# Spectral filters of a two-layer model: one 128 x 128 matrix per frequency, for all four elements together

## The chip, the core and the metric

The kernel runs on one core of a Trainium2 chip. A core has engines that run beside each other, each from its own queue in order: TensorE (PE, matrix products; the loads of its weights are shown apart as PEld), VectorE (DVE), ScalarE (ACT), GpSimd (POOL) and SyncE (SP), which here issues every DMA. PE writes to PSUM, eight banks of 512 f32 a partition; ACT or DVE copy the results out ("evict" them). All data are f32. The metric is the time of one execution on the device, in microseconds, lower being better, as the median of several runs. A profile of one execution comes with it.

## The reference, cut to what matters

The input is 4 elements ("b") of 64 x 64 positions with 128 channels. Layer 0 is a convolutional state-space block: a projection, a 3 x 3 depthwise convolution, and selective scans along four directions (256 channels, 16 states, 4096 positions each), followed by a gated norm and a projection; then a router with 64 experts. Layer 1 mixes rows and columns, and then applies spectral filters to a normed sequence `u` of 4096 positions:

```python
Vf = jnp.fft.rfft(phi, n=n, axis=0)                  # n = 8192, 16 filters
Uf_p = jnp.fft.rfft(u, n=n, axis=1)
U_plus = jnp.fft.irfft(Vf[None, :, :, None] * Uf_p[:, :, None, :], n=n, axis=1)[:, :sl]
...
out = jnp.einsum('btkd,k,kde->bte', U_plus, s, Mpp)
out = out + jnp.einsum('btkd,k,kde->bte', U_minus, s, Mpm)
```

`U_minus` is the same with every second position of `u`, and of the result, negated. So for one frequency the sum over the 16 filters and over plus and minus is one product of `u`'s spectrum (128 channels) with one complex 128 x 128 matrix, which is the same for all four elements. Four such mixtures with a Gumbel choice are added; the choice turns into a weight for each position (`wpj`, `wseg`).

## The kernel before, in words

The time is filled by the scans. An outer loop over `s` has 2048 steps: 4 elements x 4 directions x 8 chunks of 512 positions x 16 states. One step is: a broadcast load of B and C (`bc`, L1461, SP), two exponentials of 512 (`da`, L1471, ACT), a product of 1024 (`db`, L1501, DVE), two scans of 512 (`hh`, L1507, DVE), a product with C of 1024 (L1517, POOL), and eight transposes on PE that add up in PSUM (`y`, L1543).

The rest of the model is written as generators ("pieces") that yield a weight after each piece. `deal` puts pieces between the scan's instructions, twice a step, with manual dependencies that hold them at their place in each engine's queue. `WEIGHT[b]`, the total for an element, spread over all deals, sets how much is dealt at a time; `LAG` is a weight that stands for waiting. What is not yet dealt when an element's scans end is run out in a lump. `beside(b)` (L1312) lists what goes beside the scans of element b:

- b = 0: `before_scans` of elements 1, 2, 3 (norm, projection, depthwise convolution), `gate` of 0, 1, 2, and `filters` (weights of the mixture, matrices `me` and `mo`, spectra of `phi`).
- b = 1, 2, 3: for element b - 1 the stages `after_scans`, `experts_and_sums` and `to_slots` (called front stages below), and then `convolve` for 8 of the 64 groups of slots.

`to_slots(b)` (L1094) takes a short discrete Fourier transform over blocks of positions (PE, `fu_ps`, L1106) and stores the slots to DRAM (`ud`). Even and odd positions are kept apart. `convolve` (L1117) then does within each slot what the rest of a full transform would do, as a Toeplitz product: for every group of 4 slots, in four parts, it loads `slab` (the filters' values, 1 MB a part), multiplies it with `us` (PE, `cv_ps`, L1170, 64 rows, two at a time), evicts to `y`, multiplies with the 16 matrices `me` and `mo` (PE, `zq_ps`, L1191), adds the halves on POOL, turns the result (`zt_ps`, L1213) and stores it to `zd`. `from_slots(b)` (L1238) goes back (PE, `gi_ps`, L1268), scales by `wpj` and adds to `x3`, which is the output.

PSUM: the scan holds six banks for `du`, `db` and `y`; the pieces have the two others, as two single ones (`slots(2, 0)`) or, for `convolve`, as one pair (`slots(0, 1)`, `pair`).

After the last scan comes the tail. The front stages of element 3 are run there with groups 24 to 47 of `convolve` beside them, by a ratio of 3.2, in an order of PE's queue written out by hand (`behind`); then `from_slots` of 1 and 2 and the first loads of 3's with the last 16 groups; then the rest of 3's.

## Time and profile before

| | us |
|---|---|
| median of 3 runs (10947.52 to 10952.77) | 10948.95 |
| span of the profiled execution | 10931.4 |
| DVE busy (75%) | 8233.2 |
| PE busy (79%), weight loads PEld (45%) | 8642.8, 4876.0 |
| POOL busy (62%), ACT busy (57%) | 6817.4, 6232.6 |
| HBM read 1766.77 MB, written 205.52 MB | 180 GB/s over the span |

The profiled execution is one run with the profiler on; its span lies 17.6 us under the median. A line such as "L1507 DVE TENSOR_TENSOR_SCAN hh<-da,hst,db 128x512 f32 x3584 | 4392.8, 1266" says: line 1507, engine, operation, what it writes and reads, the shape, how many; busy time in us, mean ns of one. An f32 matmul leaves two records of PE, and two of PEld. Busy shares are means over stages with different limits; which wait ends last in a stage says what bounds it.

### The profile page before, as it was taken

How to read it: one execution, taken by the hardware profiler on the slowest of the kernel's cores; microseconds unless marked ns; L12 is line 12 of the kernel's file. 1: busy time of each engine (PE TensorE's matmuls, PEld its weight loads, DVE VectorE, ACT ScalarE, POOL GpSimd, SP SyncE). 2: the span in 40 equal slices, each digit the busy share in tenths (PEclk: the TensorE clock that was granted, in tenths of full speed). 3: DMA queues.
4: the chain of work that ended last, by engine and by line, in shares of the span. 5: the costliest groups of instructions: out<-in, count | busy, mean ns of one | idle time of the engine just before them, and what ended most of it. 6: DMA issues, size and time to landing. Idle time of an engine off the chain costs nothing. (4 is left out here: it accounts for less than half of the span.)

```text
span 10931.4 us, 119319 instructions
## 1 busy us (share of the span) xinstructions
PE 8642.8 (79%) x35936; PEld 4876.0 (45%) x35936; DVE 8233.2 (75%) x7094; ACT 6232.6 (57%) x12156; POOL 6817.4 (62%) x6102
## 2 busy tenths in 40 slices
PE   6787777657786777768777777787777799999999
PEld 2444444434454444445543344455344444445443
DVE  0888989988998999989989899798899922222322
ACT  4767676758576655675755557657556544134221
POOL 1777777987777887877777788677788711001000
PEclk9788888768888888878888888788788899999999
DMA  2455656657756666657565567575666565544554
GB/s 94 167 194 181 208 182 213 211 187 222 236 191 205 187 195 189 216 166 270 167 193 179 170 194 229 167 255 161 197 199 189 174 165 129 143 126 107 137 134 118
DMA packets 901464, 1980.28 MB, mean 181 GB/s; under 512 B 101562, under 2 KB 415578, under 8 KB 899290
## 3 DMA queue, kind: packets, MB, share of 16 engines
q1 hardware_dynamic: 900826, 1972.65, 59.2%
q8 instruction: 293, 4.80, 0.2%
q14 instruction: 345, 2.83, 0.1%
HBM read 1766.77 MB, written 205.52 MB: 180 GB/s over the span
## 5 line engine op out<-in xcount | busy, mean ns | idle before, releaser
L1517 POOL TENSOR_TENSOR hh<-hh,bc 128x1024 f32<-128x1024 f32 x2048 | 4885.4, 2386 | 413.6 <-DVE hh L1507 177.0
L1507 DVE TENSOR_TENSOR_SCAN hh<-da,hst,db 128x512 f32<-128x512 f32 x3584 | 4392.8, 1266 | 487.8 <-PE y L1543 134.6
L1471 ACT ACTIVATE da<-dl,aneg 128x512 f32<-128x512 f32 x4096 | 2765.9, 717 | 1845.2 <-DVE hh L1507 1769.7
L1543 PE MATMUL y<-ident,hh 128*128 128x128 f32 x16384 | 2605.4, 307 | 552.8 <-POOL hh L1517 474.7
L1543 PEld LDWEIGHTS y<-ident,hh 128*128 128x128 f32 x16384 | 2169.9, 159 | 1914.6 <-issue 1012.9
L1501 DVE TENSOR_TENSOR db<-du,bc 128x1024 f32<-128x1024 f32 x1920 | 2365.4, 1232 | 178.6 <-ACT du L1452 76.9
L1170 PE MATMUL cv_ps<-slab,us 64*128 64x512 f32 x4096 | 1162.1, 673 | 519.9 <-ACT y L257 277.7
L257 ACT COPY y<-cv_ps 128x512 f32<-128x512 f32 (+1 forms) x1024 | 755.9, 743 | 718.4 <-PE cv_ps L1170 703.1
L1516 POOL COPY hst<-hh 128x2 f32<-128x2 f32 x1792 | 381.4, 213 | 1065.8 <-DVE hh L1507 961.1
L1191 PE MATMUL zq_ps<-y,me 128*128 128x512 f32 x2048 | 998.4, 608 | 38.6 <-ACT y L257 35.3
L1191 PE MATMUL zq_ps<-y,mo 128*128 128x512 f32 x2048 | 975.9, 600 | 0.0
L1207 POOL TENSOR_TENSOR zt<-zt,zt 128x512 f32<-128x512 f32 x64 | 81.1, 1268 | 1205.9 <-DVE zt L255 608.8
L1170 PEld LDWEIGHTS cv_ps<-slab,us 64*128 64x128 f32 x4096 | 397.0, 201 | 974.3 <-ACT y L257 368.4
L255 DVE COPY y<-cv_ps 128x512 f32<-128x512 f32 x640 | 441.4, 691 | 508.3 <-PE cv_ps L1170 456.6
L1507 DVE TENSOR_TENSOR_SCAN hh<-da,db 128x512 f32<-128x512 f32 x512 | 596.7, 1207 | 41.8 <-PE y L1543 8.8
L411 PE MATMUL cv_ps<-xh,diag 128*128 128x512 f32 x1152 | 524.9, 598 | 9.4 <-ACT dl L1396 9.1
L1191 PEld LDWEIGHTS zq_ps<-y,me 128*128 128x128 f32 x2048 | 350.8, 193 | 368.1 <-issue 261.1
L1191 PEld LDWEIGHTS zq_ps<-y,mo 128*128 128x128 f32 x2048 | 359.1, 192 | 318.7 <-issue 316.6
L1361 PE MATMUL dt_ps<-dts,dtw 8*128 8x512 f32 x512 | 352.1, 801 | 160.7 <-ACT zt L257 45.3
L1501 DVE TENSOR_TENSOR db<-dx,bc 128x1024 f32<-128x1024 f32 x128 | 210.8, 1647 | 332.4 <-POOL dx L1403 319.6
L1387 POOL TENSOR_TENSOR ex<-ex,dx 128x1024 f32<-128x1024 f32 x128 | 302.5, 2363 | 159.8 <-ACT dx L1384 146.6
L255 DVE COPY zt<-zq_ps 128x512 f32<-128x512 f32 x42 | 29.0, 691 | 491.4 <-PE zq_ps L1191 491.4
(235 smaller groups left out, 9283.9 us busy)
## 6 DMA issues: line engine op xcount, KB each, us to landing
bc<-bc_d SPq DMA_DIRECT2D x2048, 512.0 KB
slab<-hd SPq DMA_DIRECT2D x1024, 256.0 KB
xc<-xc_d SPq DMA_DIRECT2D x128, 512.0 KB
y_d<-ys SPq DMA_DIRECT2D x128, 512.0 KB
w1t<-in_w_dram SPq DMA_DIRECT2D x128, 512.0 KB
w2t<-in_w_dram SPq DMA_DIRECT2D x256, 256.0 KB
xc_x<-xc_d SPq DMA_DIRECT2D x64, 512.0 KB
yk<-y_d SPq DMA_DIRECT2D x128, 256.0 KB
```

Source lines behind the costliest of these rows:

```text
L255: nc.vector.tensor_copy(dst, src)
L257: nc.scalar.copy(dst, src)
L411: nc.tensor.matmul(ps, diag[:, h, t, :], xh[:, 8 * g + dy : 8 * g + dy + 8, dx : dx + W], start=(t == 0), stop=(t == 8),)
L1170: nc.tensor.matmul(pq[q].rearrange("p (r k t) -> p r k t", r=2, t=BS), us[b, G][rows, p, a if e == 0 else 1 - a, :], slab[i][rows, p, :, : ...
L1191: nc.tensor.matmul(z, (me, mo)[e][:, KQ * kq + k, :], ys[e][:, :, :, :, k, :].rearrange("p a q r t -> p (a q r) t"), start=(e == 0 and k = ...
L1361: nc.tensor.matmul(ps, dtw[:, k, h * P : (h + 1) * P], dts, start=True, stop=True)
L1471: i_act = nc.scalar.activation(das[t][:, h, :], sizes[t // N][0][:, h, :], AF.Exp, scale=aneg[:, tk, h, t % N : t % N + 1],)
L1501: nc.vector.tensor_mul(db, src, bcs[s][:, 0:1, :].to_broadcast([P, 2, SC]))
L1507: i_dve = nc.vector.tensor_tensor_scan(o, d0, d1, init, ALU.mult, ALU.add)
L1516: nc.gpsimd.tensor_copy(hsts[t // N][:, :, t % N], hhs[t][:, :, last])
L1517: i_pool = nc.gpsimd.tensor_mul(hhs[t], hhs[t], bcs.pop(t)[:, 1:2, :].to_broadcast([P, 2, SC]))
L1543: i_pe = nc.tensor.matmul(ys[c][:, q, h, :], hhs[t][:, h, q * P : (q + 1) * P], ident, is_transpose=True, start=(n == 0 and k > 0 and q % ...
```

## The change

The blocks of even and odd positions are given up. One transform of 8192 points is split in two: over 64 blocks of 64 positions (as before in `to_slots`, now 64 slots of both halves), and within a slot over its 64 positions by a matrix with the twiddle factors in it (`fq`, `gq`, from `_twiddled`, stored in DRAM, 4.2 and 8.4 MB). `filters` now also turns the 32 matrices `me`, `mo` and stores them (`md`), and stores the filters' full spectra (`vd`, 32 x 64 x 128).

`convolve` and `from_slots` are gone, and with them the pair of banks, `behind` and the ratios. Beside the scans there are only front stages: `before_scans(3)` goes from element 0's scans to element 2's, the gates each an element ahead of their use, and `WEIGHT` is set to what these stages' own weights sum to, which is dealt over the whole of an element's scans. In the tail the front stages of element 3 run alone. Behind them, with the weights' memory freed, comes `spectrum`: for two slots at a time (`FB`, 32 iterations) it

- loads `vt`, `u1` and `fq` and transforms all four elements (`forward`),
- makes the two slots' 2 x 64 complex matrices from 32 filters (`taps_of`): 128 products of 32 rows x 256 columns, on four row groups of the array; 32 evictions of 1024, stored with a step of 512 bytes to `wt` (one buffer, 128 KB a partition),
- multiplies (`product`): 128 products with 32 columns of weights (4 frequencies x real and imaginary x 4 elements, of which 8 rows are used) and 256 columns moving, on four column groups; 8 evictions of 1024 to `zs` (one buffer), and 16 DMAs of 64 KB to `zf`,
- loads `zf` again in another order (`load_back`) and transforms back (`backward`), to `zd`.

`endings` does what `from_slots` did, for all elements at once. PSUM is held by `spectrum` as four pairs of banks. The diff follows, with the old lines of the functions that went left out:

```diff
@@ -32,47 +32,70 @@
 
 
 FIRST = 1
-WEIGHT = (1346.0, 2080.0, 1999.0, 2052.0)
+WEIGHT = (972.0, 1008.0, 1346.0, 927.0)
 
 BUSY = (2, 3)
 
 LAG = 5.0
 
-BESIDE = 8
-
-
-BS = 32
-NB = HALF // BS
+BP = 64
+NB = L // BP
 NQ = NB
-KQ = 8
+KK = 2 * KF
+FB = 2
...
-    zd = [dram.tile([NQ, 2, BS, 2, C], F32, name=f"zd{b}") for b in range(B)]
-
-    HDQ = 2 * 2 * 2 * 2 * KQ * 2 * BS
-    hd = dram.tile([NQ * HDQ + 2 * BS], F32, name="hd")
+    ud = dram.tile([NQ, 2 * BP, B, C], F32, name="ud")
+    zf = dram.tile([NQ, 2, BP, 2 * B, C], F32, name="zf")
+    zd = dram.tile([NQ, 2, BP, B, C], F32, name="zd")
+    vd = dram.tile([KK, NQ, 2 * BP], F32, name="vd")
+    md = dram.tile([KK, C, C], F32, name="md")
 
     ident = const.tile([P, P], F32, name="ident")
     make_identity(nc, ident)
...
+                me = fp.tile([P, 4, C], F32, name="me")
+                mo = fp.tile([P, 4, C], F32, name="mo")
+                nc.gpsimd.tensor_add(me, accp[:, ks], accm[:, ks])
+                nc.gpsimd.tensor_sub(mo, accp[:, ks], accm[:, ks])
+                for i in range(4):
                     for m in (me, mo):
+                        nc.scalar.activation(
+                            m[:, i], m[:, i], AF.Identity, scale=sg[:, k + i : k + i + 1]
+                        )
                 yield 3.0
+                for a, m in enumerate((me, mo)):
+                    ps = bank([P, 4, C], "mt_ps")
+                    for i in range(4):
+                        nc.tensor.transpose(ps[:, i, :], m[:, i, :], ident)
+                    mT = fp.tile([P, 4, C], F32, name="mT")
+                    evict(mT, ps)
+                    nc.sync.dma_start(
+                        md[a * KF + k : a * KF + k + 4].rearrange("k e d -> e k d"), mT
+                    )
+                    yield 2.0
...
+            for q in range(0, NQ, 4):
+                fr = hp.tile([BP, 4, 2, 2 * BP], F32, name="fr", bufs=3)
+                for i in range(4):
+                    nc.sync.dma_start(
+                        fr[:, i], fq_d[q + i].rearrange("(r p) n -> p r n", p=BP)
+                    )
+                ps = bank([KK, 4, 2 * BP], "v_ps")
+                for i in range(4):
+                    for r in range(2):
                         nc.tensor.matmul(
+                            ps[:, i, :],
+                            hs[:, q + i, r, :],
+                            fr[:, i, r, :],
+                            start=(r == 0),
+                            stop=(r == 1),
+                        )
+                vs = hp.tile([KK, 4, 2 * BP], F32, name="vs")
+                evict(vs, ps)
+                nc.sync.dma_start(vd[:, q : q + 4, :], vs)
+                yield 2.0
...
+    def spectrum():
+
+        with tc.tile_pool(name="sp", bufs=2) as sp, tc.tile_pool(
+            name="sp_ps", bufs=4, space=PSUM
+        ) as sps:
+            taps = sp.tile([P, C // 8, 2, C], F32, name="taps", bufs=1)
+            for g in range(4):
+                nc.sync.dma_start(
+                    taps[g * KK : (g + 1) * KK],
+                    md.rearrange("k (j g i) d -> k j g i d", g=4, i=2)[:, :, g],
+                )
+            wt = sp.tile([P, FB * 2 * BP, C], F32, name="wt", bufs=1)
+            u1, fq, vt, ut, zq, gq = {}, {}, {}, {}, {}, {}
+            side["e"] = 0
+
+            def banks():
+                return sps.tile([P, 2, 512], F32, name="sp_ps", tag="ps")
+
+            def out(dst, src):
+                side["e"] += 1
+                (nc.scalar.copy if side["e"] % 2 else nc.vector.tensor_copy)(dst, src)
+
+            def load(i):
+                vt[i] = sp.tile([P, FB, 2 * BP], F32, name="vt")
+                for g in range(4):
+                    nc.sync.dma_start(vt[i][g * KK : (g + 1) * KK], vd[:, FB * i : FB * (i + 1)])
+                for q in range(FB * i, FB * (i + 1)):
+                    u1[q] = sp.tile([P, B, C], F32, name="u1")
+                    nc.sync.dma_start(u1[q], ud[q])
+                    fq[q] = sp.tile([P, 2 * BP], F32, name="fq")
+                    nc.sync.dma_start(fq[q], fq_d[q])
+
+            def forward(i):
+                ps = banks()
+                ut[i] = sp.tile([P, FB, BP, 2, B], F32, name="ut")
+                for s in range(FB):
+                    q = FB * i + s
+                    for b in range(B):
+                        nc.tensor.matmul(
+                            ps[:, s, b * 2 * BP : (b + 1) * 2 * BP],
+                            u1[q][:, b, :],
+                            fq[q],
+                            start=True,
+                            stop=True,
+                        )
+                    out(
+                        ut[i][:, s].rearrange("d m u b -> d b (m u)"),
+                        ps[:, s].rearrange("d (b n) -> d b n", b=B),
                     )
 
+            def taps_of(i):
+                for j in range(C // 8):
+                    pair = [banks(), banks()]
+                    for t in range(2):
+                        for g in range(4):
+                            rows = slice(g * KK, (g + 1) * KK)
                             nc.tensor.matmul(
+                                pair[g // 2][:, g % 2, t * 256 : (t + 1) * 256],
+                                taps[rows, j, t, :],
+                                vt[i][rows].rearrange("k s n -> k (s n)"),
                                 start=True,
                                 stop=True,
                             )
+                    for h in range(2):
+                        e = 8 * j + 4 * h
+                        out(
+                            wt[:, :, e : e + 4].rearrange("d n e -> d e n"),
+                            pair[h].rearrange("d g (t n) -> d (g t) n", t=2),
+                        )
+
+            def product(i):
+                for s in range(FB):
+                    q = FB * i + s
+                    zs = sp.tile([P, BP // 4, 2, C], F32, name="zs", bufs=1)
+                    for m in range(0, BP // 4, 4):
+                        ps = banks()
+                        for k in range(4):
+                            w0 = ut[i][:, s, 4 * (m + k) : 4 * (m + k) + 4]
+                            for g in range(4):
+                                n = 2 * (s * BP + 4 * (m + k) + g)
+                                nc.tensor.matmul(
+                                    ps[32 * g : 32 * g + 32, k // 2, (k % 2) * 256 :][:, 0:256],
+                                    w0.rearrange("d m u b -> d (m u b)"),
+                                    wt[:, n : n + 2, :].rearrange("d w e -> d (w e)"),
+                                    start=True,
+                                    stop=True,
+                                )
+                        out(
+                            zs[:, m : m + 4].rearrange("z m w e -> z (m w e)"),
+                            ps.rearrange("z k n -> z (k n)"),
+                        )
+                    for g in range(4):
+                        for w in range(2):
+                            nc.sync.dma_start(
+                                zf[q, w].rearrange("(m g) z e -> z g m e", g=4)[:, g],
+                                zs[40 * g : 40 * g + 8, :, w, :],
+                            )
+
+            def load_back(i):
+                for q in range(FB * i, FB * (i + 1)):
+                    zq[q] = sp.tile([P, 2, B * C], F32, name="zq")
+                    for w in range(2):
+                        nc.sync.dma_start(
+                            zq[q][:, w], zf[q, w].rearrange("m (u b) e -> (m u) (b e)", u=2)
+                        )
+                    gq[q] = sp.tile([P, 2, 2 * BP], F32, name="gq")
+                    nc.sync.dma_start(gq[q], gq_d[q])
+
+            def backward(i):
+                ps = banks()
+                zo = sp.tile([P, FB, B * C], F32, name="zo", bufs=1)
+                for s in range(FB):
+                    q = FB * i + s
+                    for w in range(2):
                         nc.tensor.matmul(
+                            ps[:, s, :], gq[q][:, w, :], zq[q][:, w, :], start=(w == 0), stop=(w == 1)
+                        )
+                out(zo, ps)
+                for s in range(FB):
+                    nc.sync.dma_start(
+                        zd[FB * i + s].rearrange("r p b e -> (r p) (b e)"), zo[:, s, :]
+                    )
+
+            n = NQ // FB
+            load(0)
+            load(1)
+            forward(0)
+            for i in range(n):
+                if i >= 1:
+                    load_back(i - 1)
+                taps_of(i)
+                if i + 1 < n:
+                    forward(i + 1)
+                if i + 2 < n:
+                    load(i + 2)
+                if i >= 1:
+                    backward(i - 1)
+                product(i)
+            load_back(n - 1)
+            backward(n - 1)
...
             def turn(g):
                 for t in range(4):
+                    ps = gps.tile([NB, B * C], F32, name="gi_ps", tag="ps")
+                    nc.tensor.matmul(ps, gi_t, zb[g][:, t, :], start=True, stop=True)
+                    xt = xr[g][:, t].rearrange("j b c -> j (b c)")
+                    nc.vector.scalar_tensor_tensor(xt, ps, wpj, xt, ALU.mult, ALU.add)
...
     def beside(b):
 
         if b == 0:
-            for i in range(1, B):
-                yield from before_scans(i)
-            for i in range(B - 1):
-                yield from gate(i)
+            yield from before_scans(1)
+            yield from before_scans(2)
+            yield from gate(0)
+            yield from gate(1)
             yield from filters()
-        else:
-            yield from after_scans(b - 1)
-            yield from experts_and_sums(b - 1)
-            yield from to_slots(b - 1)
-            if b == 1:
-                yield from gate(B - 1)
-            if b == B - 1:
-                yield from from_slots(0)
-            yield from convolve(all_groups[BESIDE * (b - 1) : BESIDE * b])
+            return
+        if b == 2:
+            yield from before_scans(3)
+        yield from after_scans(b - 1)
+        yield from experts_and_sums(b - 1)
+        yield from to_slots(b - 1)
+        if b < B - 1:
+            yield from gate(b + 1)
...
     side["tail"] = True
-    slots(8, 0)
...
+    slots(8)
+    run(after_scans(B - 1))
+    run(experts_and_sums(B - 1))
+    run(to_slots(B - 1))
+    side.pop("pool").close()
+    weights.close()
+    spectrum()
+    endings()
```

## The prediction

> **What bounds the kernel now.** I read the page first, then busy time by stage, then the chain of waits, and at the end single tiles. The page's slices (each digit a tenth, 273 us a slice) show two regimes.
>
> ```profile
> PE   6787777657786777768777777787777799999999
> ...
> DVE  0888989988998999989989899798899922222322
> ```
>
> For 32 slices DVE is nearly full; in the last eight DVE falls to 2 and PE stands at 9. The stages come from the scan's own instructions: an element starts at 295, 2370, 4472, 6613 us, and the last scan ends at 8746. Busy time by stage (length, then PE, PEld, DVE, ACT, POOL, clock, DMA share, GB/s), and one quiet stretch:
>
> ```profile
> 295.00:2370.00 2075.00, 1519.12 (x6024) 917.18 (x6024) 1899.20 (x1560) 1419.90 (x2631) 1647.08 (x1324) 0.81 0.59 194
> 2370.00:4472.00 2102.00, 1586.92 (x7453) 971.04 (x7452) 1912.24 (x1561) 1365.06 (x2590) 1665.72 (x1435) 0.85 0.65 201
> 4472.00:6613.00 2141.00, 1588.80 (x7380) 966.37 (x7380) 1921.67 (x1562) 1328.68 (x2523) 1650.10 (x1422) 0.84 0.62 194
> 6613.00:8746.00 2133.00, 1613.32 (x7455) 984.04 (x7456) 1917.54 (x1560) 1327.93 (x2523) 1658.69 (x1449) 0.85 0.63 197
> 8746.00:10931.00 2185.00, 2130.63 (x7175) 953.68 (x7173) 578.03 (x828) 659.50 (x1577) 159.82 (x395) 0.99 0.53 132
> ...
> 8001.00:8680.00 679.00, 515.67 (x2180) 284.08 (x2180) 646.62 (x529) 412.62 (x590) 560.65 (x386) 0.88 0.63 191
> ```
>
> In the quiet stretch convolution pieces run beside the scan and DVE is busy 95%: 176 steps (three DVE instructions each) in 679 us, 3.858 us a step, 61.7 us a chunk of 16. So the filters beside the scans cost the scan nothing, and taking them out gives nothing there. At that rate 128 chunks are 7898 us, but the scans took 8746 - 295 = 8451: 553 us of stalls. They lie beside the front stages. Two samples of the waits (us in total, times, longest), 5495 to 5570 us beside `to_slots`, and 2670 to 2770 us beside the router:
>
> ```profile
> PE fu_ps L1106 <- DMA ub<-u_d: 9.7, 1, 9.7
> ...
> DVE hh L1507 <- PE y L1543: 16.9, 4, 5.8
> ...
> DVE hh L1507 <- ACT da L1471: 23.5, 5, 8.2
> ```
>
> A dealt piece waits at the head of PE or ACT for its own input; the scan's transposes or exponentials queue behind it, then DVE stops. In the tail the chain of waits is PE alone:
>
> ```profile
> 10784.63 13.93 PE zq_ps L1191 x32
> ```
>
> 32 records of 512 columns in 13.93 us: 0.435 us each, 0.85 ns a column, two records for each f32 matmul.
>
> **What the Trainium skill says.** (1) TensorEngine Tiling (Array Packing), Key Properties: tiles of the array run in parallel, a change of tiling mode drains. Before agrees for two tiles: `cv_ps` (64 rows) keeps PE busy 1162.1/4096 = 0.284 us a record against 998.4/2048 = 0.487 for `zq_ps` of full height. Four are in no row of before. (2) TensorE: Matmul & The Clock Gate, Measured speedup vs the span model: four row tiles gave 3.07x, three column tiles 2.38x. (3) The tiling page, PSUM Bottleneck: evacuation does not speed up with PE. (4) SBUF — State Buffer, the note on cachelines under Door 1: every access on a new 16-byte line pays. Before agrees:
>
> ```profile
> L429 ACT COPY byc<-sg_v x64: 1052/1094/1130, 87.6 to 1753.8; 128x512 f32<-128x512 f32 x64
> ...
> L404 ACT COPY xh<-in_ps x64: 562/588/647, 67.6 to 1627.6; 128x512 f32<-128x512 f32 x64
> ...
> L980 DVE TENSOR_REDUCE mk<-xT x4: 7097/7168/7317, 3190.0 to 9844.8; 128x64 f32<-128x4096 f32 x4
> ```
>
> The same ACT copy of 512 takes 1.09 us when its stores step by 256 bytes (`byc`) and 0.59 when they run on (`xh`): 1 ns an element more. DVE reading with that step takes 7168/4096 = 1.75 ns an element instead of about 1.04.
>
> **Part 1, the scans.** `convolve` and `from_slots(0)` leave; the front stages are dealt at a new rate. `WEIGHT` over 868 deals an element is work per deal: 1.55, 2.40, 2.30, 2.36 before, 1.12, 1.16, 1.55, 1.07 after. So a load issued some pieces ahead has twice the time in elements 1 and 3, and about 1.4 times in 0 and 2. Of 553 us of stall, some 120 are in element 0, and 27 in each of the others are DVE's own work beside the scan and stay (`mk` 7.2, MAX8 and MATCH_REPLACE8 4.4 each, 16 reductions of 0.67). I take 60, 60, 90 and 60 us after: 270. Bounds: 100 (DVE's own work and some 20) and 553 (stalls go per piece, not per rate). Scans: 7898 + 270 = 8168, a gain of 283. The filters' added work (32 transposes, 144 matmuls, 32 small activations, some 90 DMAs on SP) is dealt in element 0 beside DVE; if that cover goes it is some 30 us.
>
> **Part 2, the tail's front, now uncovered.** After the scan of the last element its front stages ran 8746 to 10134 with PE full of filters. Alone I sum the engine or queue that limits each: `after_scans` 16 groups x about 5.8 us (PE's or ACT's instructions) + fill 108; router norm 8 x 7.7 + fill 70; softmax, top-k, pooling 55; two expert loops (PE 62 and 65 us of records, 16.8 MB of weights each) 68 + 65; the second norm 80; mixing, regression 16 x 4.3 + fill 85; `to_slots` 35: 566, and a tenth for gaps and cold clock, 620. The stretch 12 to 67 us, where the first norm runs alone, took 55 us for 46 of ACT, so such stages run near their limit. Bounds 540 and 750.
>
> **Part 3, the spectrum.** 32 iterations of two slots each. PE: forward 16 records of 128 columns, 16 x 0.109 = 1.7 us; taps 256 records of 256 columns, four row tiles, 256 x 0.214/4 = 13.7; product the same in four column tiles, 13.7; backward 8 x 0.435 = 3.5. Sum 32.6, 1043 us in all: the floor. But taps has 32 evictions of 1024 elements an iteration, alternating ACT and DVE, each storing with a step of 512 bytes into `wt`. ACT: 1.02 us for 1024 (the long form of L257 reaches 1045 ns) + 1024 x 1.0 ns = 2.0; back to back some 0.1 overlaps: 1.9. DVE: 1.23 (L1501 for 1024) + 1024 x 0.7 = 1.95. 16 rounds x 1.9 = 30.5 us, PE's 13.7 beneath it. `wt` has one buffer, so the product waits for the last of them, and the next taps' stores wait for the product: the phases add.
>
> Product: slot one's 6.8 us on PE, last eviction at about 8.1; `zs` has one buffer, so slot two's evictions wait for eight stores to `zf`. SP issues one in some 0.35 us, so the last goes at about 11, and lands some 2 us later by the fixed cost that DMA: Bandwidth & Descriptors, Anatomy of one DMA, gives (an estimate): 13.5 to 14. PE has done slot two by 13.7 in the four PSUM tiles; its evictions take 2.3 more: 16.4. Forward and backward hide under the last taps evictions, with their loads issued most of an iteration ahead. Half clock at the product's start (the router stretch, PE 56% busy, was granted 0.70) about 2, semaphores about 1. Iteration: 30.5 + 16.4 + 3 = 50 us; 32 x 50 = 1600, first loads 10, last way back 20: 1630. Bounds: 39 us an iteration if scattered stores cost nothing (16 x 1.2 instead of 30.5), 70 if ACT and DVE, storing into the same lines' neighbours at once, obstruct each other, or column tiles go two at a time (27 instead of 13.7).
>
> **Part 4, endings.** 8 MB of `x3`, 16.8 MB of `zd`, 8 MB out: 33 MB at the 279 GB/s that before reached beside the experts (2810 to 2940 us), 118; DVE's 64 x 0.743 = 48 and PE's 64 x 2 x 0.435 = 56 lie beneath. Take 115.
>
> **Sum.** 295 + 8168 + 5 + 620 + 1630 + 115, and 10 for the last store = 10843 against the span of 10931. The median is 10948.95, 17.6 above the span: 10861. The tail grows from 2185 to about 2375; the scans give 283.
>
> **Rivals.** R1, scattered stores are free: 39 us, 10861 - 32 x 11 = 10510. For: no row shows DVE writing this way. Against: `byc`. R2, slower than before: the taps' scattered stores, in the phase between forward and product, take 2.3 us instead of 1.9, since both engines store at once and DVE's cost is taken from a read: 32 x 16 x 0.4 = 205, 11066. It decides from an iteration of 52.8 us (10949 - 10861 = 88, over 32), one store at 2.07. R3, the rate is not what makes the stalls; 480 of the 553 stay: 11070. For: some 27 us of element 2's stall came at 6026 to 6231 us, beside filters alone; against: the sampled waits are for latencies. R4, both work as said but PE is the bound (stores 1.0, tiles four wide): 10400.
>
> **Chances.** Forecast 0.44 (own range 10740 to 10970: mostly faster, 0.37, same 0.05, slower 0.02); R1 with R4 0.15; R2 and worse 0.26 (slower 0.23, same 0.02, faster 0.01); R3 0.15 (slower 0.10, faster 0.04, same 0.01). Faster 0.57, same 0.08, slower 0.35, within 0.2% (22 us) being what a measurement can't tell. The range takes R1 and R2 in and leaves out 70 us an iteration: 10480 to 11240.
>
> **What would show it.** Taps evictions near 2 us on ACT and DVE with PE idle between, and an iteration near 50; a gap of ACT and DVE in the middle of each product, ended by a DMA of `zf`; scans ending near 8460; the last front stages done near 9090. I am wrong if the evictions take 1.2 or over 2.3, if the four tiles' records don't start together, or if scans end after 8650.

## The result, and the profile after

The changed kernel takes 10841.51 us (median of 4 runs, 10833.02 to 10850.15), the kernel before, run beside it, 10950.86 us: a ratio of 0.9902 with a 95% interval of 0.9888 to 0.9916. The forecast was 10861 in a range of 10480 to 11240; it held. The way there was in part another than the forecast's, as the stages show.

The slices of the page, after (each digit a tenth of busy time, a slice is 271 us):

```profile
PE   7676776677676777777677767677767677777775
DVE  0899999989999999989999999999997016666663
ACT  4666666657655666767656766655565446666662
```

DVE now stands at 9 for nearly all of the scans, where before it had dropped to 8 again and again and once to 7. Then come two slices of front stages alone, and then a stage that was not there before, with PE at 7 and DVE and ACT at 6 each. No engine is full in it; they take turns.

Busy time by stage, after (length; then PE, PEld, DVE, ACT, POOL, granted clock, DMA share, GB/s). The first four rows are the scans of the elements, then the front stages of element 3, the spectrum, and the endings:

```profile
298.00:2306.00 2008.00, 1422.91 (x5820) 896.79 (x5820) 1890.98 (x1562) 1294.13 (x2319) 1595.95 (x1235) 0.76 0.59 187
2306.00:4312.00 2006.00, 1428.09 (x6675) 954.20 (x6676) 1906.62 (x1560) 1249.75 (x2475) 1581.96 (x1395) 0.78 0.61 193
4312.00:6340.00 2028.00, 1507.53 (x6971) 979.63 (x6970) 1906.52 (x1561) 1347.82 (x2759) 1611.20 (x1466) 0.81 0.63 201
6340.00:8334.00 1994.00, 1391.36 (x6523) 939.14 (x6522) 1901.84 (x1561) 1201.39 (x2384) 1563.63 (x1380) 0.78 0.59 188
8334.00:8893.00 559.00, 412.37 (x1804) 249.25 (x1804) 59.92 (x80) 243.60 (x877) 107.90 (x355) 0.75 0.44 132
8912.00:10658.00 1746.00, 1350.60 (x17142) 883.08 (x17142) 1100.21 (x687) 1070.69 (x688) 0.00 (x0) 0.94 0.29 67
10672.00:10831.00 159.00, 79.50 (x129) 21.11 (x128) 48.77 (x65) 0.00 (x0) 0.00 (x0) 0.75 0.91 215
```

An element's scans take about 2000 us in place of 2075 to 2141, with DVE's busy time the same: what went is waiting. The scans end at 8334 instead of 8746, 412 us earlier; from there to the end it is now 2497 us instead of 2185, 312 more. The change is these two against each other.

The shares of the chain of waits by line, after, in which the tail that had been PE alone has become a mixture:

```profile
ACT wt L1184 4%; DVE wt L1184 4%; PE sp_ps L1244 2%; SPq L1257 2%; PE sp_ps L1220 1%; DMA zf<-zs 1%; PE sp_ps L1278 1%; ACT zs L1184 0%; PE gi_ps L1331 0%; PE sp_ps L1202 0%; PE h_ps L941 0%; DMA zb<-zd 0%; PE fu_ps L1152 0%; DVE zs L1184 0%; PE ar_ps L1099 0%
```

The taps evictions (`wt`) carry some 8% of the span, nearly half of the spectrum; SP's issuing of stores (SPq L1257, `zf`) 2%. The groups behind these, after (busy us, mean ns of one, then idle time before it and what ended most of it):

```profile
L1184 ACT COPY wt<-sp_ps 128x1024 f32<-128x1024 f32 x512 | 896.4, 1934 | 50.6 <-PE sp_ps L1220 49.4
L1184 DVE COPY wt<-sp_ps 128x1024 f32<-128x1024 f32 x512 | 896.3, 1891 | 33.2 <-PE sp_ps L1220 32.7
L1184 DVE COPY zs<-sp_ps 128x1024 f32<-128x1024 f32 x128 | 153.7, 1222 | 516.5 <-DMA zf<-zs 353.0
L1184 ACT COPY zs<-sp_ps 128x1024 f32<-128x1024 f32 x128 | 126.4, 1014 | 532.7 <-DMA zf<-zs 358.7
```

The same line with the same shapes takes 1934 and 1891 ns where it stores with a step (`wt`), 1014 and 1222 where it stores in a run (`zs`). The records of `wt` overlap: 896.4 us of busy time for 512 of them are 1.75 us each, and in the run of them their starts lie 1.73 us apart on both engines. The 350 us of idle time before the `zs` copies, ended by the DMA of `zf`, are the wait for the one buffer.

One iteration of the 32 in the timeline, after (start, length, engine, line, what, and in brackets the idle time before it and what ended it); the taps lie between the first two lines and the third:

```profile
9132.15 27.90 DVE L1184 COPY wt<-sp_ps 128x1024 f32<-128x1024 f32 x16 [0.80 <-PE sp_ps L1220]
9132.40 27.90 ACT L1184 COPY wt<-sp_ps 128x1024 f32<-128x1024 f32 x16 [1.52 <-PE sp_ps L1220]
...
9161.01 1.16 PE L1202 MATMUL sp_ps<-fq,u 128*128 128x128 f32 x8 [0.65 <-DVE ut L1184]
9162.01 2.74 PE L1278 MATMUL sp_ps<-zq,gq 128*128 128x512 f32 x6
...
9164.68 14.02 PE L1244 MATMUL sp_ps<-wt,ut 128*32 128x256 f32 x256
...
9173.15 6.83 SPq L1257 DMA_DIRECT2D zf<-zs  x8
...
9183.34 1.93 ACT L1184 COPY zs<-sp_ps 128x1024 f32<-128x1024 f32 x2 [12.20 <-DMA zf<-zs]
```

From the first taps matmul at 9130.02 to the next one at 9184.41 it is 54.39 us: 30.3 until the last taps eviction ends, 4.4 in which PE runs the rest of forward and backward and nothing lies over it, 14.0 of product, and 5.7 in which PE stands still. PE stands still because SP needs 6.83 us to issue the eight stores of the first slot, and only when the last has landed may the second slot's evictions write `zs` and free the PSUM tiles for the next taps. The 31 iterations take 54.54 us in the mean.

### The profile page after: what moved, and what is told of

It reads as the page before. It is cut to its first block, busy times and chain, and to the rows that moved or that the text cites. A ratio compares the mean times of both kernels' runs of the same rounds, so it can differ in the third digit from the quotient of the medians.

```text
span 10831.2 us, 137865 instructions
## 1 busy us (share of the span) xinstructions
PE 7804.8 (72%) x45520; PEld 5010.1 (46%) x45520; DVE 8819.7 (81%) x7100; ACT 6539.7 (60%) x11814; POOL 6496.7 (60%) x5909
## 5 line engine op out<-in xcount | busy, mean ns | idle before, releaser
L1573 PE MATMUL y<-ident,hh 128*128 128x128 f32 x16384 | 2754.9, 323 | 1690.6 <-POOL hh L1547 1562.6
L1220 PE MATMUL sp_ps<-vt,taps 32*128 32x256 f32 x8192 | 720.1, 439 | 354.8 <-ACT zs L1184 173.1
L1184 ACT COPY wt<-sp_ps 128x1024 f32<-128x1024 f32 x512 | 896.4, 1934 | 50.6 <-PE sp_ps L1220 49.4
L1184 DVE COPY wt<-sp_ps 128x1024 f32<-128x1024 f32 x512 | 896.3, 1891 | 33.2 <-PE sp_ps L1220 32.7
L1220 PEld LDWEIGHTS sp_ps<-vt,taps 32*128 32x128 f32 x8192 | 519.1, 208 | 557.6 <-ACT wt L1184 193.8
L1184 DVE COPY zs<-sp_ps 128x1024 f32<-128x1024 f32 x128 | 153.7, 1222 | 516.5 <-DMA zf<-zs 353.0
L1244 PE MATMUL sp_ps<-wt,ut 128*32 128x256 f32 x8192 | 449.2, 379 | 0.7 <-DVE wt L1184 0.7
L1184 ACT COPY zs<-sp_ps 128x1024 f32<-128x1024 f32 x128 | 126.4, 1014 | 532.7 <-DMA zf<-zs 358.7
L1430 PE MATMUL dl_ps<-ex,ident 128*128 128x512 f32 x512 | 310.6, 695 | 111.6 <-POOL ex L1424 111.6
L1244 PEld LDWEIGHTS sp_ps<-wt,ut 128*32 128x32 f32 x8192 | 263.1, 110 | 194.8 <-issue 23.5
L1433 POOL TENSOR_TENSOR dx<-dl,xc 128x1024 f32<-128x1024 f32 x128 | 302.4, 2363 | 84.2 <-ACT dl L1431 75.3
```

Source lines behind the costliest of these rows:

```text
L1184: (nc.scalar.copy if side["e"] % 2 else nc.vector.tensor_copy)(dst, src)
L1220: nc.tensor.matmul(pair[g // 2][:, g % 2, t * 256 : (t + 1) * 256], taps[rows, j, t, :], vt[i][rows].rearrange("k s n -> k (s n)"), start= ...
L1244: nc.tensor.matmul(ps[32 * g : 32 * g + 32, k // 2, (k % 2) * 256 :][:, 0:256], w0.rearrange("d m u b -> d (m u b)"), wt[:, n : n + 2, :]. ...
L1430: nc.tensor.matmul(ps, ident, t[:, h], start=t is dl, stop=t is w)
L1573: i_pe = nc.tensor.matmul(ys[c][:, q, h, :], hhs[t][:, h, q * P : (q + 1) * P], ident, is_transpose=True, start=(n == 0 and k > 0 and q % ...
```

## The experiments

The kernel before, run beside each group of these variants, took 10938 to 10946 us (10951 beside the change); ratios are to it. Differences between variants are taken from medians, so between groups some 10 us can't be told.

### Rate or filters: e4_oldrate

The gain beside the scans has two possible sources: no filters dealt there any more, or a lower rate of dealing. Only the rate is set back.

```diff
-WEIGHT = (972.0, 1008.0, 1346.0, 927.0)
+WEIGHT = (1346.0, 2080.0, 1999.0, 2052.0)
```

> Changed kernel with the old numbers in WEIGHT (1346, 2080, 1999, 2052), so that the front stages are dealt 1.4 to 2.2 times as fast and end in the first part of an element; filters stay behind the scans. Theory (the rate makes the stalls of the scans): stalls of 136 us return to 350 to 450, scans end near 8550 to 8650 instead of 8334, time 11050 to 11150. Rival (it was the convolution's pieces beside the scans that made the stalls): stalls stay under 170 us, time within 30 us of 10841.

11245.91 us (11238.01 to 11248.19), ratio 1.027 (1.0252 to 1.0287): 404 us slower than the change, and more than was expected. DVE's last scan ends at 8740, as before (8742; 8331 in the change). What the steps took beyond the quiet step (61.7/16, 3.856 us each) sums to 114, 106, 198, 127 us in the four elements, 545 in all, where before had 553 and the change has 34, 31, 54, 16, that is 135. The spectrum's iteration is 54.64 us, unchanged.

What DVE waited for in the scans of element 1 (us in total, times, longest), with the old rate:

```profile
DVE hh L1537 <- ACT da L1501: 31.7, 9, 8.1
DVE db L1531 <- ACT du L1482: 14.9, 4, 5.9
DVE hh L1537 <- PE y L1573: 13.1, 6, 4.5
DVE hh L1537 <- ACT uo L268: 9.8, 2, 8.5
```

and with the change's rate:

```profile
DVE hh L1537 <- PE y L1573: 5.9, 1, 5.9
DVE db L1531 <- DMA bc<-bc_d: 5.2, 3, 3.1
...
DVE hh L1537 <- ACT da L1501: 0.5, 1, 0.5
```

The reader is to see the exponentials (`da`): with the old rate DVE waits for them nine times and up to 8.1 us, as it would if dealt pieces that wait for their own input stood ahead of them in ACT's queue; with the new rate once, for half a microsecond. (Before had 24.6 us of this wait in the same element, seven times.) So the rate makes all of the scans' gain, and that the filters went from beside the scans gave them nothing by itself: with them gone and the old rate there is no gain at all, and the longer tail then makes the kernel slower than before. What the filters' going can have done is to leave room for the lower rate; the kernel before with a lower rate was not run.

### Stores with a step, or so many stores: e2_order and e3_contig

The taps evictions went element by element of `wt`'s last dimension, so every store stepped by 512 bytes. The same 1024 values go to the same places in another order: four neighbours (16 bytes), then the step. The step of 1 KB is then on the side of the PSUM read.

```diff
-                            wt[:, :, e : e + 4].rearrange("d n e -> d e n"),
-                            pair[h].rearrange("d g (t n) -> d (g t) n", t=2),
+                            wt[:, :, e : e + 4],
+                            pair[h].rearrange("d g (t n) -> d n (g t)", t=2),
```

> Changed kernel; the taps evictions walk the same elements in another order: the four neighbours of a line innermost instead of the 256 lines, so that successive stores fill 16 bytes before they step by 512; PSUM is then read with a step of 1 KB. Theory (the step between successive stores makes them 1.9 us): ACT near 1.05 us and DVE near 1.25, taps phase 28 to 18 us, about 32 x 10 = 320 us less, 10500 to 10560. Rival (the number of lines touched counts, whatever the order, or PSUM's strided read costs as much as the store did): 1.7 to 2.0 us as before, and the time within 1% of 10841.

The bound for it stores all 1024 in one run; the matrices then don't lie where the product looks for them, and only the time of the stores counts:

```diff
+                            wt[:, 8 * (2 * j + h) : 8 * (2 * j + h) + 8, :].rearrange("d n e -> d (n e)"),
+                            pair[h].rearrange("d g n -> d (g n)"),
```

> Changed kernel; the taps evictions store their 1024 elements in one run each, so the matrices lie in wt in the wrong places; nothing else is changed. Measures the eviction without any step: theory (the step alone makes the cost) 1.01 us on ACT and 1.22 on DVE, as for zs of the same size, and 27 x 0.8 = some 300 us less or more than that if the product starts before the last eviction. Rival (PSUM reads of two banks while PE writes the others, or ACT and DVE together, make it slow): 1.5 us or more.

e2_order took 10587.81 us (10586.99 to 10601.19), ratio 0.9674 (0.9659 to 0.9688), 254 us less than the change; e3_contig, a single run, 10585.72. The groups of e2_order:

```profile
L1184 DVE COPY wt<-sp_ps 128x1024 f32<-128x1024 f32 x512 | 609.5, 1222 | 67.9 <-PE sp_ps L1220 49.0
L1184 ACT COPY wt<-sp_ps 128x1024 f32<-128x1024 f32 x512 | 516.3, 1012 | 166.3 <-PE sp_ps L1220 147.6
```

and of e3_contig:

```profile
L1184 DVE COPY wt<-sp_ps 128x1024 f32<-128x1024 f32 x512 | 610.5, 1222 | 66.3 <-PE sp_ps L1220 48.6
L1184 ACT COPY wt<-sp_ps 128x1024 f32<-128x1024 f32 x512 | 516.6, 1012 | 165.4 <-PE sp_ps L1220 147.8
```

Four neighbours at a time cost exactly what a run costs: 1012 ns on ACT and 1222 on DVE. The penalty of 0.9 and 0.67 us was the order alone. It is what the Trainium skill, SBUF — State Buffer (the note on cachelines under Door 1), leads one to expect, that up to four f32 in a line of 16 bytes go at full rate and a new line at every access pays; these rows put the price on it. By the length of a record it is 0.90 ns an element on ACT ((1934 - 1012) / 1024) and 0.65 on DVE. By busy time for each store, in which the overlap is left out, it is at most 0.73 and 0.55: 1.75 us on both in place of 516.3/512 = 1.01 and 609.5/512 = 1.19. The taps phase, from the first eviction to the end of the last, fell from 28.3 to 20.4 us in the mean, by 8 us where 10 were expected. From the fourth round on a round takes 1.23 us, which is DVE's eviction of 1.22 back to back; since a round needs both of its tiles free, the slower engine sets the pace, and 16 times the 1.25 expected for DVE would have been 20, not 18.

### One zs buffer: e1_zs2

```diff
-                    zs = sp.tile([P, BP // 4, 2, C], F32, name="zs", bufs=1)
+                    zs = sp.tile([P, BP // 4, 2, C], F32, name="zs", bufs=2)
```

> Changed kernel with two buffers for zs. Theory (the single buffer costs a stall in the middle of every product): in an iteration of 54.6 us ACT and DVE stand still from 42.8 to 53.4 us after its start, waiting for the eight stores to zf, while PE is done at 48.8. With two buffers the last evictions end near 50.3 instead of 55.5, and the next taps can start then: 49.5 to 50.5 us an iteration, 32 x 4.5 = 145 us less, 10680 to 10720. Rival (SP's issue of these stores, 6.8 us for eight, is the limit, or PSUM is short): the wait moves to the next product or to PSUM, less than 30 us gained.

10625.12 us (10618.3 to 10627.74), ratio 0.9704 (0.969 to 0.9718): 216 us less than the change. An iteration is 47.84 us, 6.7 less and some 2 better than expected. From its timeline:

```profile
9140.80 14.02 PE L1244 MATMUL sp_ps<-wt,ut 128*32 128x256 f32 x256
...
9149.27 13.89 SPq L1257 DMA_DIRECT2D zf<-zs  x16
...
9154.75 2.55 PE L1220 MATMUL sp_ps<-vt,taps 32*128 32x256 f32 x32
```

SP still needs 13.89 us for sixteen stores, but nobody waits for it: PE's product ends at 9154.82 and the next taps begin at once, where the change had 5.6 us of standstill. The rest of the gain is that the refilling of the two evicting engines now overlaps the last `zs` evictions.

### Forward and backward under the taps evictions: e5_fwd, then e9_split

The prediction had these hide under the taps evictions. In the change PE runs them at the end of the taps, 4.4 us bare. Here they are handed out earlier:

```diff
                 for j in range(C // 8):
+                    if j == 5 and i + 1 < NQ // FB:
+                        forward(i + 1)
+                    if j == 10 and i >= 1:
+                        backward(i - 1)
```

> Changed kernel; forward of the next pair of slots is put behind the fifth round of taps and backward of the pair before behind the tenth, instead of both behind the last. Theory (they lie bare between taps and product, 4.4 us of 54.6): they go beneath taps, whose evictions leave PE idle, and cost there only their own three evictions, some 1.7 us an engine: 2.5 to 3 us an iteration, 80 to 95 us less, 10745 to 10765. Rival (the two PSUM tiles that they take stop the taps for as long): within 20 us of 10841.

10940.52 us (10932.67 to 10951.81), ratio 1.0002 (0.9994 to 1.0011): 99 us slower than the change. The theory fell, and the loss is larger than the rival had it. From its timeline, around the forward:

```profile
9154.41 5.36 ACT L1184 COPY wt<-sp_ps 128x1024 f32<-128x1024 f32 x3 [0.35 <-PE sp_ps L1224]
...
9157.92 1.16 PE L1202 MATMUL sp_ps<-fq,u 128*128 128x128 f32 x8 [0.44 <-DVE wt L1184]
...
9159.47 1.04 DVE L1184 COPY ut<-sp_ps 128x512 f32<-128x512 f32 x1
9160.56 1.16 PE L1202 MATMUL sp_ps<-fq,u 128*128 128x128 f32 x8 [0.85 <-DVE ut L1184]
...
9162.83 8.83 ACT L1184 COPY wt<-sp_ps 128x1024 f32<-128x1024 f32 x5
```

ACT ends a taps eviction at 9154.41 + 5.36 = 9159.77 and begins the next at 9162.83: 3 us lost, of which its own share of the forward, a copy of 1.07, is a third. The second slot's matmuls wait for the first slot's eviction, for both use one PSUM tile, and the taps stand behind them on PE. At the backward it is 2.7 us. That fits two pairs of PSUM tiles, which give the evictions one pair of lead and not more: what PE does between two pairs is paid but for its own slack, some 0.34 us a round in the change.

A second try cuts the same work to single slots, each with a PSUM tile of its own:

```diff
-            def forward(i):
-                ps = banks()
...
+            def forward(i, slots=range(FB)):
+                for s in slots:
+                    ps = banks()
...
+                    if j in (3, 6) and i + 1 < NQ // FB:
+                        forward(i + 1, [(3, 6).index(j)])
+                    if j in (9, 12) and i >= 1:
+                        backward(i - 1, [(9, 12).index(j)])
```

> The changed kernel with the forward and the backward matmuls handed out one slot at a time among the taps (the two forward slots ahead of taps steps 3 and 6, the two backward slots ahead of 9 and 12), each with a PSUM tile of its own. Theory: e5_fwd lost because one forward of two slots in one PSUM tile makes TensorE wait in line for its own eviction, and because 2.3 to 3.7 us of matmuls at once are more than the one pair of tiles of lead that the two evicting engines have, so that they run dry about 3 us at each of the two places. In single slots without the inner wait they run dry less than 1 us at each of four places: taps phase 30 to 32.5 us in place of 35.7, an iteration 51.5 to 54, the time 10740 to 10830. Rival (PE in order: matmuls put among the taps are always paid in full, however cut): the iteration stays at 56 to 58 as in e5_fwd, the time 10890 to 10950.

10902.98 us (10897.69 to 10920.34), ratio 0.9968 (0.9954 to 0.9982), an iteration of 56.53: 1.3 better than e5_fwd, still 2.0 worse than the change, and what the rival expected (56 to 58, 10890 to 10950). The time from the first taps to the product is 35.4 us (37.5 in e5_fwd, 34.9 in the change): cut small, the matmuls cost among the taps about what they cost behind them. But the product itself became longer. In the change every one after the first takes 14.0 us on PE; in e9_split 23 of 31 take 15 to 17, mean 15.44, in e5_fwd 14 of 31, mean 14.73. Windows of e9_split: the first 4 us and the rest of a product of 14.0, then of one of 15.7:

```profile
9508.61:9512.60 3.99, 3.99 (x76) 2.94 (x80) 0.22 (x1) 1.01 (x1) 0.00 (x0) 1.00 0.03 8
9512.60:9522.60 10.00, 10.00 (x188) 6.98 (x180) 2.23 (x2) 1.02 (x1) 0.00 (x0) 1.00 0.21 30
9564.17:9568.16 3.99, 3.98 (x48) 2.60 (x52) 0.00 (x0) 1.01 (x1) 0.00 (x0) 0.64 0.04 12
9568.16:9579.80 11.64, 11.64 (x212) 8.19 (x204) 2.45 (x2) 1.01 (x1) 0.00 (x0) 0.98 0.17 23
```

The clock is the third figure from the right. In the longer product's first 4 us only 48 records passed in place of 76. Cut where the grant changes, the same product reads:

```profile
9561.89:9565.30 3.41, 1.12 (x24) 0.86 (x27) 2.14 (x2) 2.08 (x2) 0.00 (x0) 1.00 0.14 39
9565.30:9568.71 3.41, 3.41 (x40) 2.13 (x36) 0.00 (x0) 1.01 (x1) 0.00 (x0) 0.50 0.02 5
9568.71:9572.12 3.41, 3.41 (x69) 2.48 (x65) 1.23 (x1) 0.81 (x1) 0.00 (x0) 1.00 0.00 0
```

A stretch of 3.41 us in which PE was busy for 1.12 is followed by one of 3.41 us at half clock, though PE is then busy throughout. Ahead of each product PE now waits 2.4 us for the last taps evictions to end; in the change it goes from backward into the product without a pause, and no product loses its clock. So the forward and the backward at the end of the taps, bare as they are, fill that pause and keep the clock up.

The pause was 2.4 us ahead of the slow products and of the quick ones alike. The Trainium skill, TensorE: Matmul & The Clock Gate (What's actually happening), has the clock follow activity in free-running windows of about 3.4 us, which would let the same pause decide differently from one iteration to the next. The trace agrees: in e9_split the recorded grant is only ever half or full, and every stretch of it is a multiple of 3.413 us on one grid. Where a product starts in that grid tells the slow from the quick: the 13 that start 0.58 to 1.17 us ahead of the next edge take 15.7 us, the 8 that start 1.76 to 2.12 ahead take 14.0, the 10 that start 2.25 to 2.74 ahead take 15.3 to 16.9. In e5_fwd the 17 quick ones lie at 1.39 to 1.93 and the 14 slow ones all outside; in e7_best, with a shorter pause, the groups overlap. The page lets the clock fall after an idle window; here a pause of 2.4 us, shorter than a window, was enough. That is read from the traces; no run was made to shift a product against the grid.

The ledger of e9_split closes: 0.6 us from taps to product, 1.4 of product, 2.0 in all.

### The endings: e8_ends

`x3` and the output move in runs of 512 bytes. The tile is laid out so that four positions are neighbours, 2 KB a run.

```diff
-                xr[g] = gp.tile([NB, 4, B, C], F32, name="xr3", bufs=6)
+                xr[g] = gp.tile([NB, B, 4, C], F32, name="xr3", bufs=6)
...
-                    nc.sync.dma_start(xr[g][:, :, b, :], mine(x3_d, b, g))
+                    nc.sync.dma_start(xr[g][:, b], mine(x3_d, b, g))
```

> Changed kernel; only the endings differ: the tile of x3 is laid out by element, so that its loads and the stores of the output are runs of 2 KB instead of 512 bytes. Theory (the endings are bound by DMA engines, 91% busy at 215 GB/s, and 512-byte packets take 43% of that): from the end of backward to the end of the program 159 us become 130 to 145. Rival (8 KB packets of zb at 560 ns each, that is HBM or the SBUF side, set it): 150 or more.

A single run, 10820.3 us. The endings fell from 159 to 151 us, short of the 130 to 145 that were expected and within what the rival had. The DMA queues in the quiet middle of the endings (10690 to 10810 us), the change:

```profile
DMA packets 26844, 26.64 MB, mean 222 GB/s; under 512 B 1897, under 2 KB 25041, under 8 KB 25041
```

and e8_ends:

```profile
DMA packets 10267, 28.65 MB, mean 239 GB/s; under 512 B 2056, under 2 KB 2056, under 8 KB 8344
```

The packets fell to 10267 from 26844, and the rate rose by 8% only. Over the endings the engines are busy 0.91 of the time in the change and 0.84 here; the rate of 279 GB/s that before reached beside the experts' weights isn't reached here. The packets in the traces speak for the rival. The 8 KB packets of `zb`, which this edit leaves as they are, take half of the engines' time in both: 562 ns each in the change and 544 here, some 15 bytes a ns. Those of `x3` and the output take 105 ns for 2 KB here, where four of 512 bytes took 135. In that stretch of before 2 KB packets took 86 ns and 4 KB ones 212, that is 24 and 19 bytes a ns. Smaller packets for `zb` were not tried.

### Together: e6_zs2_order, e7_best, e10_three, e11_three_split

> Changed kernel with both two buffers for zs and the other order of the taps evictions. If the two costs are separate stretches of the same chain, the gains add: 54.5 - 6.7 - 7.7 = 40.1 us an iteration, 10841 - 216 - 253 = 10372, 10350 to 10400. If the eight stores that take SP 6.8 us, twice an iteration, become the limit once the iteration is shorter, less: 43 us or more, over 10460.

> e6 with forward and backward among the taps as in e5, and the endings with runs of 2 KB instead of 512 bytes in their loads and stores of x3 and the output. Taps 20 us with 5.2 us of PE put in, of which PE had some 6 idle: 22 to 24; product 14; refill 2: 38 to 39 us an iteration, 30 to 60 less than e6, and 15 to 30 less in the endings: 10290 to 10330. Rival (taps are bound by the round trip between PE and the evictions, so what is put in is added in full): iteration as in e6, 10350.

e6_zs2_order (two `zs` buffers and the new order) took 10368.49 us (10361.83 to 10373.17), ratio 0.9479 (0.9465 to 0.9493). The two gains add: 10841.5 - 216.4 - 253.7 = 10371.4. An iteration is 39.9 us. Of its timeline,

```profile
9133.41 14.02 PE L1244 MATMUL sp_ps<-wt,ut 128*32 128x256 f32 x256
...
9147.36 4.74 PE L1220 MATMUL sp_ps<-vt,taps 32*128 32x256 f32 x64
...
9148.55 19.57 DVE L1184 COPY wt<-sp_ps 128x1024 f32<-128x1024 f32 x16 [1.54 <-PE sp_ps L1220]
...
9152.28 2.28 PE L1220 MATMUL sp_ps<-vt,taps 32*128 32x256 f32 x32 [0.18 <-DVE wt L1184]
```

PE goes from product to taps without a gap. In the taps DVE's 16 evictions stand back to back, 1.22 us each, and set the pace, but PE is nearly level with them: a round of 1.23 us leaves it 0.09 to wait, for DVE. In the rest of the iteration PE is the bound. e7_best adds e5_fwd's order and e8_ends' layout: 10444.94 (10431.07 to 10447.14), ratio 0.955 (0.9534 to 0.9566), 76 us slower than e6_zs2_order, where a gain was expected. Its expectation still had the forward and the backward among the taps as a gain; from the first taps to the product it is 28.0 us instead of 25.9, and 9 of 31 products lose their clock.

> The changed kernel with two zs buffers, the taps evictions in the neighbour-first order, and the 2 KB runs in the endings; the forward and the backward left where the change has them. If the parts add: 10368 (e6_zs2_order) less the 8 to 13 us that e8_ends took from the endings, 10353 to 10366. If 10370 or more, the endings' gain is not there once the spectrum is shorter.

> e10_three with the forward and backward in single slots among the taps as in e9_split. With the cheap evictions TensorE sets the taps phase (1.29 us a pair of tiles of which its matmuls fill most), so matmuls put among the taps have no idle time to go into: no gain beyond the 0.6 us of inner wait and about 1 us of drain of an iteration, 10310 to 10370. If the time falls below 10290, TensorE was waiting more than that in the taps phase.

e10_three took 10367.12 us (10359.24 to 10374.28), ratio 0.9473 (0.9459 to 0.9487), equal to e6_zs2_order within what can be told: the endings' few microseconds don't show in the sum. e11_three_split took 10402.9 (10391.51 to 10411.05), ratio 0.9505 (0.9491 to 0.9519), 36 us slower, where no loss was expected: its iteration is 40.95 us against 39.87, all of it between first taps and product (27.0 against 25.9). The matmuls found no idle time on PE to go into, and taken out of the end they leave it a pause of 1.4 us, as in e7_best. None of its products lost its clock. The best version found is the change with two edits, `zs` in two buffers and the evictions in the neighbours' order: 5.2% under the kernel before, where the change as it stands has 1.0%.

## Why the prediction was right, and where it was not

The sum was right to 12 us of span (10831.2 against 10843; the median lies 10.3 us above it, where 17.6 had been taken) by luck: four terms were off, and their errors cancelled.

- **Scans, 295 to 8468: 134 us too long.** The mechanism was right, and e4_oldrate shows it to be the only one: a lower rate, fewer stalls. The term that was mis-sized is the stalls left, 270 predicted and 135 measured. The prediction had 27 us of DVE's own work in each element "stay" as stall; element 3 has 16 us in all and the same work. DVE was busy 95% in the quiet stretch of before, which leaves it some 99 us in an element's 512 steps (5% of 1974 us), so that the own work fits in. The 135 lie within its bounds, 100 to 553. Of the 553 of before, 101 lay in element 0 (2075 us less 1974), not some 120. R3, that the rate is not what makes the stalls, is refuted.
- **Front stages alone, 620: 61 us too long.** The sum of limits was 566, and the stage took 559. The terms fit singly as well: `after_scans` took 125 us where 108 was summed, the others lie between 11 less and 1 more. The tenth added for gaps was not there.
- **Spectrum, 1630: 149 us too short** (1779 from the last front stage to the end of the last backward). The single eviction was right: 2.0 us on ACT and 1.95 on DVE predicted, 1.934 and 1.891 measured. Its phase came out as predicted, 30.5 us until the last of them ended, but by two errors: a round took 1.73 us and not 1.9, and before the first eviction lay 2.1 us in which PE fills the first tiles, which the sum did not have. (The plain rate of about 1.04 ns that DVE's term starts from stands in none of the lines shown; copies of 1024 elements in 1222 ns, `zs`, and of 512 in 691, `y` at L255 of before, give it.) Two other steps failed. "Forward and backward hide under the last taps evictions": they don't, 4.4 us an iteration, and e5_fwd and e9_split show that neither of two ways to move them beneath pays. And "SP issues one in some 0.35 us": eight took 6.8 us, 0.85 each. The 2 us to landing were a second error: the section of the Trainium skill that they are taken from (DMA: Bandwidth & Descriptors, Anatomy of one DMA) is on DMAs that POOL issues, and here, where SP issues them, 3.4 us passed from the end of the last issue to the next eviction. So the product phase with its wait was 19.6 us instead of 16.4. The wait itself, at the place and for the DMA that the prediction named, is there, and e1_zs2 shows it to be worth 216 us. The 3 us for a cold clock and semaphores were not needed: the product runs at a clock of 1.00, and in e5_fwd and e9_split, where the bare forward and backward do not lie ahead of it, 14 and 23 of 31 don't. The sum is 4.4 + 3.2 - 3.0 = 4.6 us, by which 54.5 exceeds the 49.9 of the prediction's terms.
- **Endings, 125 with the last store: 34 us too short.** They move their data at 215 GB/s, not at the 279 taken from another stage, which moved other packets (e8_ends). At 279 its own sum was 118, and it took 115.

The rival R2 was given as decisive from an iteration of 52.8 us. The iteration passed that mark, not by dearer stores (1.93 and 1.89 us, below the 2.07 that R2 needed) but by the two failed steps; the kernel is faster all the same since scans and front stages came out 195 us shorter than in the sum. R1, that stores with a step are free, is refuted by e2_order in the plainest way. R4, that PE is the bound, was not the change's case; e6_zs2_order comes near it, with PE level with DVE in the taps and the bound elsewhere: 10368, where R4 gave 10400.

## What to carry to other kernels

Where one dealt piece after another stalls a loop that sets the time, first look at how fast they are dealt: spreading the same pieces over the whole of the loop was worth 400 us here, and taking other work out from between them nothing by itself. In a scattered eviction choose the order so that neighbours of 16 bytes are stored together; the step then belongs on the PSUM side. Before moving matmuls under an engine's evictions count the PSUM tiles of lead, and ask what pause of PE they fill where they are: in e9_split the clock lost behind the pause cost 1.4 us an iteration, and the move lost more than it gained.

## What the runs showed of the hardware

- ACT and DVE read PSUM with a step of 1 KB at the full rate of a contiguous read (e2_order and e3_contig, 1012 and 1222 ns for 1024 elements in both).
- ACT and DVE storing 1024 f32 with a step of 512 bytes took 1.93 and 1.89 us; the same stores with four neighbours first took 1.01 and 1.22, as long as 1024 stored without any step (the change, e2_order, e3_contig).
- Four column tiles run truly side by side: 256 product records of 256 columns in 14.02 us, 55 ns each, where the full-height rate of before (0.435 us for 512 columns) gives 218 ns for one; a factor of 4.0. The Trainium skill, TensorE: Matmul & The Clock Gate (Measured speedup vs the span model), has 2.38 for three. The four row tiles of the taps reach 71 ns (32 records in 2.28 us, in e6_zs2_order, where PE still waits a little for DVE), a factor of 3.05 or more, where the page has 3.07.
- A store of 64 KB that leaves from 8 partitions keeps SP's queue 0.85 us in the mean, where the `ud` loads of the same queue mostly take 0.32 to 0.42. In a group of eight the first two take 0.3 us each and the later ones up to 1.4.
- A pause of PE of 2.4 us was followed by half clock for 2.6 to 6.0 us of the product in 23 of 31 iterations and by full clock in the others (e9_split). A pause of 1.4 us was so in 9 of 31 (e7_best) and in none (e11_three_split).
- In the endings 8 KB packets took 562 ns, 2 KB ones 105 (e8_ends) and 512-byte ones 34: the largest were not the quickest for their bytes.
